# Spreading ScalarE's work on the next pair's samples over more attention steps, and asking for its function tables early

One core of a Trainium2 chip; the metric is the device time of one execution, in microseconds (us). Engines are named as in the profile: PE is TensorE, DVE VectorE, ACT ScalarE, POOL GpSimd. All runs quoted are of the fast state.

## What is computed

Four layers on x of shape (2, 512, 32, 32). The change touches the first, a deformable attention whose bias is a small network over every (query, key) pair. Cut to what matters:

```python
off  = gelu(conv6x6(q) + b);  off = tanh(off @ pw) * 4        # per pair of heads: 64 sample points
kv   = grid_sample(xn, grid + off)                            # bilinear samples  -> "samples"
pos  = grid_q - grid_kv
bias = sign(pos) * log1p(abs(pos))                            # Sign, Abs, Ln
bias = relu(bias @ cpb_w1); bias = relu(bias @ cpb_w2)        # 128 x 128, for 1024 x 64 pairs a head
sim  = q @ k + bias @ cpb_w3
out  = softmax(sim) @ v                                       # Exp
```

The other three layers (an MLP with Gelu and three ordinary attentions) come after it, and the change does not touch them.

## The kernel before

The attention runs over 8 pairs of heads (t), each in 64 steps. A step fills two z tiles (16 matmuls) and evacuates both with ACT. The work of the *next* pairs is a chain of Python generators, `behind`: after each step's z work, one `next(behind)` emits what stands up to the next `yield`. In the traces ACT runs its instructions in the order in which the program emits them (h at 494.94 us, near at 496.05, wx at 497.18, wy at 497.68, the next h at 498.81), so whatever is emitted there stands on ACT between the last evacuation of this step and the first of the next.

```python
ps_s = ...tile_pool(name="att_ps_s", bufs=1, space=PSUM)   # sim
ps_z = ...tile_pool(name="att_ps_z", bufs=3, space=PSUM)   # z, and every other PSUM tile of the attention
def zt(shape, name): return ps_z.tile(shape, F32, name=name, tag="z")

def second(h1s):                                 # one step
    for part in range(2):
        z = zt([P, HW], "z")
        ...                                      # 8 matmuls in the trace (4 pairs) of 128x512
        h2 = ...
        nc.scalar.activation(h2, z, AF.Relu, bias=b2h[:, part:part+1])      # "h<-z"

def offsets(t):
    qpad = one.tile([P, 36, 36], F32, name="qpad", tag="pixels")
    nc.gpsimd.memset(qpad, 0.0)
    ...                                          # pq -> qpad, 36 taps on DVE over 24 steps
    for h in range(2): nc.scalar.activation(act[r, r], accf[r], AF.Gelu, ...)
    yield
    po = zt([P, 2], "po"); ...; nc.scalar.activation(th, po, AF.Tanh)
    yield
    ...                                          # nxy, pos, gp on DVE
    yield
    nc.scalar.activation(sgn, pos, AF.Sign); nc.scalar.activation(pos, pos, AF.Abs)
    nc.scalar.activation(pos, pos, AF.Ln, bias=1.0)
    yield

def samples(t):
    gpb = zt([P, 2, P], "gpb"); ...              # holds a z buffer
    yield
    for ax in range(2):
        nc.scalar.activation(near[:, ax, :], ir, AF.Abs, ...)
        nc.scalar.activation(near[:, ax, :], near[:, ax, :], AF.Relu, ..., accum_out=...)
    nc.vector.tensor_mul(wsum[:, 2:3], wsum[:, 0:1], wsum[:, 1:2])
    nc.scalar.activation(wx, gpb[:, 0, :], AF.Abs, bias=cs("px"))
    nc.scalar.activation(wx, wx, AF.Relu, bias=1.0, scale=-1.0)
    for k in range(8):
        nc.scalar.activation(wy[:, k, :], gpb[:, 1, :], AF.Abs, bias=cs("py", k))
        if k % 4 == 3: yield
    nc.scalar.activation(wy, wy, AF.Relu, bias=1.0, scale=-1.0)
    ...

def finish(t, sim):
    nc.scalar.activation(simb, sim, AF.Identity, bias=simbias[t])
    yield
    pt = zt([P, 8, P], "pt"); ...                # 8 transposes; holds a z buffer
    nc.vector.tensor_reduce(mx, ptv, AX.X, ALU.max, negate=True)
    yield
    for g in range(16):
        nc.scalar.activation(atv[:, g, :], ptv[:, g, :], AF.Exp, bias=mx[:, g:g+1], accum_out=...)
        if g % 4 == 3: yield
    ...
```

Of the kernel before, what the change touches and what calls it, by code (L numbers as in the profile page):

```python
# [11 lines left out]
F32 = mybir.dt.float32  # L12
AF = mybir.ActivationFunctionType
# [5 lines left out]
P = 128  # L19
# [60 lines left out]
def kernel(ctx: ExitStack, tc: tile.TileContext, a: dict, out: bass.AP):  # L80
    nc = tc.nc
# [10 lines left out]
    def col(name, i=0, n=1):  # L92
        lo = _PC_AT[name][0] + i
        return pc[:, lo : lo + n]

    def cs(name, i=None):
        lo, hi = _CONST_AT[name]
        return cst[:, lo:hi] if i is None else cst[:, lo + i : lo + i + 1]
# [34 lines left out]
    def accumulate(pm, pairs):  # L133
        for k, (w, m) in enumerate(pairs):
            nc.tensor.matmul(pm, w, m, start=(k == 0), stop=(k == len(pairs) - 1))  # L135

    def layer0(l0, fold_d, t2_b, o2_b):

        l0.enter_context(in_order(tc))
        one = l0.enter_context(tc.tile_pool(name="att1", bufs=1))  # L140
# [9 lines left out]
        def zt(shape, name):  # L150
            return ps_z.tile(shape, F32, name=name, tag="z")
# [100 lines left out]
            nc.vector.tensor_tensor(cpb_w2, cpb_w2, pw3, ALU.mult)  # L252


        gps = {}

        def offsets(t):
            b, pr = divmod(t, NPAIR)
            qpad = one.tile([P, 36, 36], F32, name="qpad", tag="pixels")
            nc.gpsimd.memset(qpad, 0.0)  # L260
            pq = zt([P, HW], "pq")
            for half in range(2):
                n = slice(half * HALF, (half + 1) * HALF)
                nc.tensor.matmul(pq[:, n], qws[:, pr, :], xs[b][:, pr, n], start=True, stop=True)
            yield
            nc.scalar.activation(
                qpad[:, 1:33, 1:33], pq.rearrange("p (y x) -> p y x", x=W), AF.Identity, bias=qb[:, pr : pr + 1]
            )
            yield

            qv = qpad.rearrange("p (a i) (c k) -> p a i c k", i=4, k=4)
            acc = one.tile([P, HD, WD], F32, name="acc")
            for tap in range(36):
                ky, kx = divmod(tap, 6)
                src = qv[:, ky // 4 : ky // 4 + HD, ky % 4, kx // 4 : kx // 4 + WD, kx % 4]
                w = col("dw_w", tap)
                if tap == 0:
                    nc.vector.tensor_scalar(acc, src, w, None, ALU.mult)
                else:
                    nc.vector.scalar_tensor_tensor(acc, src, w, acc, ALU.mult, ALU.add)  # L280
                if tap % 3 != 1:
                    yield
            accf = acc.rearrange("p y x -> p (y x)")
            act = actbd[t % 2]
            for h in range(2):
                r = slice(h * DH, (h + 1) * DH)
                nc.scalar.activation(act[r, r], accf[r], AF.Gelu, bias=col("dw_b")[r])
            yield
            po = zt([P, 2], "po")
            nc.tensor.matmul(po, act, col("pw_w", 0, 2), start=True, stop=True)  # L290
            th = two.tile([P, 2], F32, name="th")
            nc.scalar.activation(th, po, AF.Tanh)
            yield

            nxy = two.tile([P, 2], F32, name="nxy")
            nc.vector.scalar_tensor_tensor(nxy, th, 4.0, cs("gxy"), ALU.mult, ALU.add)
            nc.vector.tensor_scalar(nxy, nxy, 2.0 / 7.0, -1.0, ALU.mult, ALU.add)

            pos = two.tile([P, 2, 32], F32, name="pos")
            nc.vector.tensor_tensor(  # L300
                pos,
                cs("gq").unsqueeze(1).to_broadcast([P, 2, 32]),
                nxy.unsqueeze(2).to_broadcast([P, 2, 32]),
                ALU.subtract,
            )
            gp = two.tile([P, 2], F32, name="gp")
            nc.vector.tensor_scalar(gp, nxy, 1.0, W / 2.0, ALU.add, ALU.mult)
            nc.vector.tensor_scalar(gp, gp, -0.5, None, ALU.add)
            gps[t] = gp
            yield  # L310
            sgn = two.tile([P, 2, 32], F32, name="sgn")
            nc.scalar.activation(sgn, pos, AF.Sign)
            nc.scalar.activation(pos, pos, AF.Abs)
            nc.scalar.activation(pos, pos, AF.Ln, bias=1.0)
            yield
            nc.vector.tensor_mul(pos, pos, sgn)
            nc.sync.dma_start(out=slog_d[t].rearrange("x p i -> p x i"), in_=pos)
            tables.add(t)
# [12 lines left out]
        def samples(t):  # L331
            b, pr = divmod(t, NPAIR)
            xt = one.tile([P, 8, P], F32, name="xt", tag="pixels")
            nc.sync.dma_start(
                out=xt, in_=a["xt"][b, :, pr * P : (pr + 1) * P].rearrange("(k p) c -> p k c", p=P)
            )

            gp = gps.pop(t)
            gpb = zt([P, 2, P], "gpb")
            for ax in range(2):  # L340
                nc.tensor.matmul(
                    gpb[:, ax, :], gp[:, ax : ax + 1].to_broadcast([P, P]), ident, start=True, stop=True
                )
            yield

            near = two.tile([P, 2, 32], F32, name="near")
            wsum = two.tile([P, 3], F32, name="wsum")
            for ax in range(2):
                nc.scalar.activation(near[:, ax, :], ir, AF.Abs, bias=gp[:, ax : ax + 1], scale=-1.0)
                nc.scalar.activation(  # L350
                    near[:, ax, :], near[:, ax, :], AF.Relu, bias=1.0, scale=-1.0, accum_out=wsum[:, ax : ax + 1]
                )
            nc.vector.tensor_mul(wsum[:, 2:3], wsum[:, 0:1], wsum[:, 1:2])
            wx = one.tile([P, P], F32, name="wx")
            nc.scalar.activation(wx, gpb[:, 0, :], AF.Abs, bias=cs("px"))
            nc.scalar.activation(wx, wx, AF.Relu, bias=1.0, scale=-1.0)
            wy = one.tile([P, 8, P], F32, name="wy")
            for k in range(8):
                nc.scalar.activation(wy[:, k, :], gpb[:, 1, :], AF.Abs, bias=cs("py", k))
                if k % 4 == 3:  # L360
                    yield
            nc.scalar.activation(wy, wy, AF.Relu, bias=1.0, scale=-1.0)
            yield
            nc.gpsimd.tensor_tensor(wy, wy, wx.unsqueeze(1).to_broadcast([P, 8, P]), ALU.mult)
            for _ in range(4):
                yield

            pk = zt([P, 2, P], "pk")
            accumulate(pk[:, 0, :], [(xt[:, k, :], wy[:, k, :]) for k in range(8)])
            accumulate(pk[:, 1, :], [(wsum[:, 2:3].to_broadcast([P, P]), ident)])  # L370
            yield
            shift = one.tile([P, P], F32, name="shift")
            nc.scalar.mul(shift, pk[:, 1, :], col("bn1_b", pr))
            kv = kvbd[t % 2]
            for h in range(2):
                r = slice(h * DH, (h + 1) * DH)
                nc.vector.scalar_tensor_tensor(
                    kv[r, r], pk[r, 0, r], s1[r, pr : pr + 1], shift[r, r], ALU.mult, ALU.add
                )
            yield  # L380
            pkv = zt([P, 2, P], "pkv")
            nc.tensor.matmul(pkv[:, 0, :], kq_w[:, pr, :], kv, start=True, stop=True)
            nc.tensor.matmul(pkv[:, 1, :], kv, bd["vw"][:, pr, :], start=True, stop=True)
            kq = one.tile([P, P], F32, name="kq")
            nc.scalar.copy(kq, pkv[:, 0, :])
            kqs[t] = two.tile([P, P], F32, name="kqs")
            nc.scalar.mul(kqs[t], pkv[:, 0, :], s1q[:, pr : pr + 1])
            vbd[t] = two.tile([P, P], F32, name="vbd")
            nc.scalar.copy(vbd[t], pkv[:, 1, :])
            yield  # L390
            pb = zt([P, 1], "pb")
            nc.tensor.matmul(pb, kq, b1q[:, pr : pr + 1], start=True, stop=True)
            simbias[t] = two.tile([P, 1], F32, name="simbias")
            nc.vector.tensor_add(simbias[t], pb, col("cpb_b3"))
# [86 lines left out]
        def finish(t, sim):  # L481
# [5 lines left out]
            simb = two.tile([P, HW], F32, name="simb", tag="simb")  # L487
            nc.scalar.activation(simb, sim, AF.Identity, bias=simbias[t])
            yield
            pt = zt([P, 8, P], "pt")  # L490
            for i in range(8):
                nc.tensor.transpose(pt[:, i, :], simb[:, i * P : (i + 1) * P], ident)
# [93 lines left out]
        key_steps = key_weights()  # L586
        advance(key_steps)
        steps = offsets(0)
        advance(steps, 26)
        drain(key_steps)  # L590
# [736 lines left out]
    with ExitStack() as l0:  # L1327
        w1 = layer0(l0, fold_d, t2_b, o2_b)
# [92 lines left out]
```

## Time and profile before

| | before |
|---|---|
| median of 3 runs | 3727.63 us (3726.69 to 3728.03) |
| PE busy | 3675.3 of 3725.8 us |
| attention of layer 0, first to last z matmul | 55.4 to 2205.1 us |
| PE's waits of z for ACT's evacuation | 26.6 us, 23 times |

The share of busy time says that PE is full; it does not say what a change can still win. That stands in the list of PE's waits, and the chain of work shows where each wait sits: as long as PE bounds, the chain is one long piece "PE z", and where ACT lines break into it, PE stood still. The prediction shows those lines.

### The profile page before, as it was taken

The page shows a single profiled execution, that of the slowest core. Times are in us where ns is not written, and L with a number is a line of the kernel's source. Part 1 is how long each engine was busy: PE and PEld are TensorE (multiplying, and loading weights), DVE is VectorE, ACT ScalarE, POOL GpSimd, SP SyncE. Part 2 cuts the span into 40 slices and gives each one's busy share as a digit, 9 for nine tenths or more (in the row PEclk, how much of TensorE's full clock was granted, in tenths as well). Part 3 has the DMA queues.
Part 4 walks back from the last instruction along what each step waited for, and adds up shares of the span by engine and source line. Part 5 has one row for each costly group of instructions (what it writes and reads, how often), then busy time and mean ns, then how long its engine had stood idle before and what let it go on. Part 6 is the DMA issues. An engine that isn't in the chain of part 4 may idle for free.

```text
span 3725.8 us, 37390 instructions
## 1 busy us (share of the span) xinstructions
PE 3675.3 (99%) x15234; PEld 1342.1 (36%) x15234; DVE 2371.8 (64%) x2317; ACT 1586.4 (43%) x1940; POOL 478.6 (13%) x188
## 2 busy tenths in 40 slices
PE   9999999999999999999999999999999999999999
PEld 4333333333333333333333334444433333444443
DVE  6988998998996998998998960000036447030222
ACT  4655566565664566656656541100134234111111
POOL 1112122122121012121132210000001000000000
PEclk9999999999999999999999999999999999999999
DMA  4100012001010110010101001000100000000000
GB/s 149 24 15 14 18 24 62 17 20 18 18 23 12 13 23 18 18 24 12 24 18 22 18 2 51 9 34 12 57 1 1 1 1 0 14 0 0 6 29 24
DMA packets 96852, 78.42 MB, mean 21 GB/s; under 512 B 10656, under 2 KB 84768, under 8 KB 95904
## 3 DMA queue, kind: packets, MB, share of 16 engines
q1 hardware_dynamic: 96528, 75.41, 8.3%
q8 instruction: 123, 2.02, 0.2%
q14 instruction: 57, 0.47, 0.0%
q10 hardware_dynamic: 144, 0.52, 0.0%
HBM read 64.12 MB, written 10.75 MB: 20 GB/s over the span
## 4 chain that ended last, share of the span: by engine, by line
PE 93%; DVE 3%; ACT 3%; issue 0%; DMA 0%; POOL 0%; SPq 0%; DVEq 0%; POOLq 0%; ACTq 0%
PE z L443 44%; PE sim L465 6%; PE pw L135 6%; PE ph L991 6%; PE pp L1002 6%; PE pm L1026 5%; PE pmv L135 4%; PE score L1130 3%; PE score L135 3%; PE pv L1178 3%; PE ppr L1057 2%; PE pp L549 1%; ACT h L451 1%; DVE h L425 1%; DVE h L456 1%; PE pf L135 1%
## 5 line engine op out<-in xcount | busy, mean ns | idle before, releaser
L443 PE MATMUL z<-h,cpb_w 128*64 128x512 f32 x8192 | 1788.7, 594 | 28.5 <-ACT h L451 26.6
L451 ACT ACTIVATE h<-z,b2h 128x1024 f32<-128x1024 f32 x1024 | 1137.8, 1114 | 868.0 <-PE z L443 858.7
L425 DVE CUSTOM_DVE_ANT_1 h<-tab,tab 128x1024 f32<-128x1024 f32 x1024 | 1221.8, 1234 | 121.1 <-PE z L443 120.7
L443 PEld LDWEIGHTS z<-h,cpb_w 128*64 128x64 f32 x8192 | 575.6, 137 | 1208.9 <-issue 1107.5
L456 DVE SCALAR_TENSOR_TENSOR h<-h,turn,h 128x1024 f32<-128x1024 f32 x512 | 689.6, 1347 | 5.3 <-ACT h L451 5.3
L410 POOL TENSOR_SCALAR tab<-tab,pc 128x512 f32<-128x512 f32 x63 | 270.9, 4300 | 1576.3 <-DMA tab<-slog_d 1116.3
L1005 DVE SCALAR_TENSOR_TENSOR x<-pp,pc,x 128x512 f32<-128x512 f32 x16 | 12.0, 749 | 375.8 <-PE pp L1002 375.8
L465 PE MATMUL sim<-h,w 128*32 128x512 f32 x2048 | 234.3, 595 | 0.7 <-DVE h L456 0.7
L135 PE MATMUL pw<-p,vT 128*128 128x512 f32 x512 | 221.8, 593 | 1.3 <-DVE y L1236 1.3
L991 PE MATMUL ph<-xn,wa 128*128 128x512 f32 x512 | 220.9, 593 | 1.4 <-POOL xn L975 1.4
L1002 PE MATMUL pp<-hid,wb 128*128 128x512 f32 x512 | 220.4, 592 | 0.0
L1131 ACT ACTIVATE p<-score 128x1024 f32<-128x1024 f32 x144 | 139.5, 1021 | 156.8 <-PE score L1130 156.8
L1068 DVE TENSOR_TENSOR acc<-acc,p 128x2048 f32<-128x2048 f32 x56 | 129.6, 2315 | 105.1 <-ACT p L1131 57.8
L994 ACT ACTIVATE hid<-ph,pc 128x512 f32<-128x512 f32 x64 | 44.0, 687 | 332.6 <-PE ph L991 332.6
L953 POOL TENSOR_SCALAR hc<-x,sc,sh 128x1024 f32<-128x1024 f32 x16 | 29.0, 1822 | 902.3 <-DVE sh L949 870.1
L1070 DVE TENSOR_TENSOR acc<-p 128x2048 f32<-128x2048 f32 x12 | 27.5, 2291 | 182.2 <-ACT p L1265 108.8
L991 PEld LDWEIGHTS ph<-xn,wa 128*128 128x128 f32 x512 | 97.1, 190 | 123.2 <-issue 120.4
L1002 PEld LDWEIGHTS pp<-hid,wb 128*128 128x128 f32 x512 | 97.4, 190 | 122.4 <-issue 122.4
L135 PEld LDWEIGHTS pw<-p,vT 128*128 128x128 f32 x512 | 97.1, 190 | 122.5 <-issue 120.9
L411 POOL TENSOR_SCALAR tab<-tab,pc 128x512 f32<-128x512 f32 x63 | 131.1, 2081 | 16.3 <-DMA tab<-slog_d 16.2
L1130 PE MATMUL score<-q,k 64*128 64x512 f32 x512 | 127.2, 615 | 0.0
L1026 PE MATMUL pm<-hc,wa 128*64 128x512 f32 x512 | 122.5, 604 | 0.0
(217 smaller groups left out, 2044.5 us busy)
## 6 DMA issues: line engine op xcount, KB each, us to landing
tab<-slog_d SPq DMA_DIRECT2D x128, 256.0 KB, 6.3
wa<-in_qkv_w SPq DMA_DIRECT2D x8, 768.0 KB, 6.8
xt<-in_xt SPq DMA_DIRECT2D x8, 512.0 KB, 3.8
wa<-in_mlp_w SPq DMA_DIRECT2D x4, 1024.0 KB, 17.0
wb<-in_mlp_w SPq DMA_DIRECT2D x16, 256.0 KB, 5.4
x_d<-x SPq DMA_DIRECT2D x16, 256.0 KB, 2.0
out<-x SPq DMA_DIRECT2D x16, 256.0 KB, 2.0
wa<-in_proj_w SPq DMA_DIRECT2D x8, 256.0 KB, 9.0
```

The source lines that it names most:

```text
L135: nc.tensor.matmul(pm, w, m, start=(k == 0), stop=(k == len(pairs) - 1))
L410: engine.tensor_scalar(tabs[0], tabs[0], col("cpb_w1", 0), col("cpb_b1"), ALU.mult, ALU.add)
L425: nc.vector._custom_dve(TENSOR_ADD_SAT, out=h1, in0=tx[:, quad, ri, :].unsqueeze(1).to_broadcast([P, H, W]), in1=ty[:, quad, ri, :].unsque ...
L443: nc.tensor.matmul(z[point * 64 : point * 64 + 64, n], cpb_w2[:, part * 64 : part * 64 + 64], h1s[point][:, n], start=True, stop=True,)
L451: nc.scalar.activation(h2, z, AF.Relu, bias=b2h[:, part : part + 1])
L456: nc.vector.scalar_tensor_tensor(parts[0], parts[0], turn, parts[1], ALU.mult, ALU.add)
L465: nc.tensor.matmul(sim[quad * 32 : quad * 32 + 32, n], w3[:, lo : lo + 32], h2[:, n], start=(r == 0 and j < 4), stop=False,)
L991: nc.tensor.matmul(ph, w1[:, k, m * P : (m + 1) * P], xn_now[:, k, :], start=(k == 0), stop=(k == CC - 1))
L1002: nc.tensor.matmul(pp, w2[:, k, m * P : (m + 1) * P], h1[:, k, :], start=(k == 0), stop=(k == HID // P - 1))
L1026: nc.tensor.matmul(pm[at : at + wide], w[:, k, lo + at : lo + at + wide], h[k][:, n], start=(k == 0), stop=(k == CC - 1),)
L1130: nc.tensor.matmul(sc[:, part, :], ks[part][r, left[part]], qs[part][r, n], start=True, stop=True)
L1131: nc.scalar.activation(p[:, :, n], sc, AF.Exp, scale=scale)
```

## The change

Its intent: ACT's stretches of work between two evacuations become shorter, so that none is long enough to let PE run out of free z buffers. The samples' activations are spread over five steps in place of three. The tables for Gelu, Ln and Exp are asked for one to three steps ahead, by a one-column activation on a scratch tile, `table(...)`, before which the compiler puts the table load.

```diff
+        trial = one.tile([P, 2], F32, name="trial")
+        nc.gpsimd.memset(trial, 1.0)
+
+        def table(function):
+            nc.scalar.activation(trial[:, 1:2], trial[:, 0:1], function)
 ...  offsets(t)
+                if tap == 33:
+                    table(AF.Gelu)
                 if tap % 3 != 1:
                     yield
 ...
             gps[t] = gp
+            table(AF.Ln)
             yield
 ...  samples(t)
             nc.vector.tensor_mul(wsum[:, 2:3], wsum[:, 0:1], wsum[:, 1:2])
+            yield
             wx = one.tile([P, P], F32, name="wx")
 ...
-                if k % 4 == 3:
+                if k % 3 == 1:
                     yield
 ...  finish(t, sim)
             yield
+            table(AF.Exp)
             pt = zt([P, 8, P], "pt")
```

## The prediction

> **What bounds the kernel now.** I read the page's busy shares first, then the slices, the view of who waited for whom, the chain that ended last in two short windows, and the groups of ScalarE.
>
> TensorE (PE) is busy 3675.3 of 3725.8 us, so in the whole program only about 50 us can be won by filling its gaps. The change touches the first part alone, the bias attention of layer 0 (55 to 2206 us, 512 steps of two z tiles each). The waits of PE, longest first, begin so:
>
> ```profile
> PE z L443 <- ACT h L451: 26.6, 23, 1.6
> PE den L1085 <- DVE acc L1068: 3.4, 2, 2.2
> PE den L135 <- ACT r L1100: 2.7, 4, 0.7
> PE pwarm L160 <- ACT warm L157: 2.3, 1, 2.3
> PE z L443 <- ACT qpad L266: 1.9, 1, 1.9
> ```
>
> Columns: total us, times, longest. 23 waits of the z matmuls for ScalarE's (ACT) evacuation h carry more than half of all PE idle time; nothing else in the attention comes near. Where are they? The chain that ended last shows two kinds in one period of 266.7 us (one of the eight pairs of heads). The first is in the samples:
>
> ```profile
> 491.28 3.63 PE z L443 x16
> 494.92 0.02 issue
> 494.94 1.11 ACT h L451
> 496.05 0.22 ACT near L349
> ...
> 497.18 0.26 ACT wx L355
> ...
> 497.68 1.12 ACT wy L359 x4
> 498.81 1.01 ACT h L451
> 499.82 0.04 issue
> ```
>
> Between two evacuations ACT does near, wx and four wy; PE sits until the h after them frees a z buffer, at 499.86. The second is in the softmax (start us, us, what):
>
> ```profile
> 603.70 1.11 ACT h L451
> 604.82 0.02 issue
> 604.83 1.28 ACT L501
> 606.12 0.01 issue
> 606.13 1.02 ACT at L501 x7
> ...
> 607.42 1.01 ACT h L451
> 608.43 0.04 issue
> ```
>
> "ACT L501" with no tile is the table load for Exp. A third, the same with Gelu's load at 473.36 and two Gelu activations, is in the offsets. The groups of ACT count the loads that the change is about:
>
> ```profile
> L314 ACT ACT_TABLE_LOAD x8 | 10.3, 1283 | 0.1
> L287 ACT ACT_TABLE_LOAD x7 | 9.0, 1283 | 0.1
> L501 ACT ACT_TABLE_LOAD x7 | 9.0, 1283 | 0.1
> ```
>
> I then read the timeline at each place and took the distance between starts of neighbouring PE matmuls over the usual 0.43 us: samples 8 times 1.73 us; Exp 7 times 1.58, and 0.16 once more in its later steps; Gelu 6 times 0.79 (the seventh falls beside the sim matmuls); Ln 2 times 0.33. Sum 13.8 + 12.2 + 4.7 + 0.7 = 31.4 us. The wait list agrees: 26.6 us, plus 23 times 0.163 us, because a matmul's modelled 0.592 us overhangs its 0.43 us spacing, plus the seven small ones of 0.16, is 31.5. That is the ceiling of the gain: 0.84% of the time.
>
> **What the Trainium skill says.** "ScalarE: Activation LUTs", section "What ACT_TABLE_LOAD costs", gives about 1283 ns for the load and about 1380 ns of drain with it. The trace agrees on the load (1283 ns) but shows no drain: load at 604.83, next activation at 606.13. So I charge 1.28 us for a load. The same page, "Table sets: the hidden batching unit", says that cheap functions such as relu, copy, identity and abs are in every set; in the trace h (Relu) runs between loads without a reload, so a load asked for two steps early is not undone by the h in between. "PSUM — Partial Sum Buffer", "Specifications (TRN2)", has eight banks of 512 fp32 per partition: a z tile of 1024 takes two, the program has three z buffers and one sim, and the memory is full. "Perfetto Trace Analysis", "Optimization Strategy", reads consistent bubbles as a lack of buffers: here the bubbles recur at the same three places of each period.
>
> **How a stall arises.** PE fills a z tile in 1.72 us (128 matmuls, 16 tiles, take 27.62 us, less 0.16 of overhang). h starts 0.23 us after the fill, runs 1.11, and PE goes on 0.06 later: 1.40 us from fill to free. ACT is idle 0.60 us between two h. With three buffers PE may run two fills on, so the slack is 3.43 - 1.40 = 2.03, and extra work X between two h stalls PE only if it exceeds 0.60 + 2.03 = 2.63 us. But gpb, pt and po are tiles of the same three buffers, and while one lives the slack is 1.72 - 1.40 = 0.32: X may be 0.92. Check on before: samples X = 2.73 gives 1.81 (read: 1.73); Exp X = 2.5 gives 1.6 (read: 1.58). So the size of X and the state of the buffers explain what I see.
>
> **The change, part by part.** Built, both programs have the same number of table loads; the changed one gains 24 one-column activations (8 each of Gelu, Ln, Exp, some 0.2 us by the 0.17 to 0.25 of ACT's smallest rows) and one small memset; PE, VectorE (DVE) and the queues keep their instructions, later by two steps from wy on.
>
> 1. Samples. The 2.73 us become 1.14 (near), 1.12 (wx, two wy), 0.8 and 0.8 (three wy each), one group a step, gpb held two steps longer. First group: 1.14 - 0.92, about 0.2 of stall. That stall shifts PE against ACT, so the second group, no larger, adds nothing; a step has 3.43 us for 2.23 of h, so 1.20 is free and every group fits. Left 0.2 of 1.73: saved 1.5 x 8 = 12.2.
> 2. Exp. The load goes one step up, where pt is not yet taken and PE's eight transposes (1.02 us) give ACT more room: ACT was idle 1.78 us there. X = 1.5, no stall. Each of the four steps keeps X = 1.2 with pt held: 2.23 + 1.2 is just the step, so some 0.2 at the first and the 0.16 of before at a later one remain, about 0.4 of 1.74. Saved 1.3 x 7 = 9.3, just the load.
> 3. Gelu. Load plus trial, X = 1.5, two steps ahead with three buffers: under 2.63. Then X = 0.7 with po: under 0.92. Saved 0.75 x 6 = 4.5.
> 4. Ln: likewise 0.6 in all. In the prologue PE is busy with the folds up to the first z at 55.36, so nothing there; the last pair's Exp needs no load before or after.
>
> Sum: 12.2 + 9.3 + 4.5 + 0.6 = 26.6 us. All lie on PE, which is the chain, so they count in full: 3727.6 - 26.6 = 3701. As nearly every unforeseen thing makes it less, I say 3702.
>
> **The rivals.** *VectorE becomes the bound.* In the period from 606.5 to 873.2 us DVE is busy 244.85 of 266.70 us; with PE's period shortened by 3.6 it would be 93%. Over the taps of the offsets DVE needs more per step (3.7 plus half a us) than PE gives (3.9 with sim's share), and its lead before the z matmuls, read as the distance from the end of h1 to PE's start, sinks from over 5 to 1.7 us there, and to 1.4 us after the samples; one could fear that 1.5 us less of PE stall makes it nil. Against it: before the taps DVE waits for PE for 6.4 us at 630 to 641, so it starts them with full buffers anyhow; and the 2.1 us that GpSimd's wy product costs DVE (one 3.38 us join at 773.19) comes two steps later too. If it does bite, up to 1 us a period comes back: 3710. *The wait only moves.* ACT has the same work and 24 trials more. If my thresholds were wrong by half a us, each early load would stall PE by that; 22 of them, 11 us: 3712. The check of the thresholds at two places speaks against it, and ACT is busy only 160.68 us of the 266.70. *gpb held longer makes a new wait.* Two more steps on two buffers, perhaps 0.2 each: 3 us, 3705. *All stalls go*: 3696, which needs the Exp steps to fit with no rest.
>
> **Range and chances.** 3702 us, 8 in 10 between 3698 and 3710: the low end is nearly no rest at the samples and Exp, the high end is DVE biting in each period. The ceiling of 31.4 us is 0.84%, so a gain over 2% is excluded by the trace as I read it, and a loss over 2% would need 3.3 us of new stall at each of the 22 places. Faster 0.01, same 0.98, slower 0.01.
>
> **What would show it.** Right: PE's wait of z for h falls from 26.6 us to 2 to 5, PE idle by some 23; the period becomes about 263.1 us; table loads still 8, 7, 7 but before tile trial; PE goes without a gap past wx and past the Exp load, with rests of about 0.2 at near and the first exp. Wrong: z waits on DVE h L425, or sim on the join, of more than 2 us in total (the first rival); gaps beside the trial loads (the second); gaps of 0.2 or more at each wy group (the third); a load more than before per period.

## The result

| | before | after |
|---|---|---|
| median | 3727.4 us (4 runs, 3726.69 to 3728.03) | 3701.84 us (4 runs, 3700.96 to 3704.68) |
| ratio of fast runs | | 0.9933, 95% interval 0.9916 to 0.995 |
| the same again, other chip time | 3727.97 us (9 runs) | 3701.4 us (5 runs), ratio 0.993 |

Ratios are the mean time of one kernel's fast runs over that of the other's of the same rounds, so not quite the ratio of the medians quoted. 25.6 us were saved (26.6 the second time), under the 2% line: "same" by verdict, and 3701.84 against 3702 predicted.

PE's waits in the changed kernel, in the same view that opened the prediction (total us, times, longest):

```profile
PE z L454 <- ACT qpad L273: 3.5, 1, 3.5
PE den L1097 <- DVE acc L1080: 3.4, 2, 2.2
```

The line of 26.6 us is gone whole, and no wait for a DVE tile took its place. The groups of ACT now hold the loads under the line of `table`:

```profile
L259 ACT ACT_TABLE_LOAD x22 | 28.2, 1283 | 0.4
L259 ACT ACTIVATE trial<-trial 128x1 f32<-128x1 f32 x24 | 4.8, 202 | 0.2
```

22 loads as before (8 + 7 + 7), of the same 1283 ns, and 24 trials of 0.2 us: 4.8 us more on ACT, though its busy time in the page grows by 1.9 only (1586.4 to 1588.3). No wait of PE in the list is for them. The chain that ended last, in the windows that hold Exp's load and the Gelu, Ln and samples of one period:

```profile
596.44 1.02 PE pt L504 x8
597.47 14.74 PE z L454 x65
...
738.26 0.31 PE po L299 x2
738.57 10.45 PE z L454 x48
749.02 0.64 PE gpb L351 x4
749.66 3.57 PE sim L476 x32
753.23 21.77 PE z L454 x100
```

Where ACT lines broke into the chain before (Exp's load, near to wy), PE now runs through. ACT around Exp's load, in the timeline (start, duration, idle before):

```profile
596.49 1.11 ACT L462 ACTIVATE h<-z,b2h 128x1024 f32<-128x1024 f32 x1 [0.28 <-PE z L454]
597.62 1.28 ACT L259 ACT_TABLE_LOAD   x1
598.92 0.20 ACT L259 ACTIVATE trial<-trial 128x1 f32<-128x1 f32 x1
599.38 1.11 ACT L462 ACTIVATE h<-z,b2h 128x1024 f32<-128x1024 f32 x1 [0.26 <-PE z L454]
```

The load fits between two evacuations, with 0.26 us to spare before the next z is full: the time in which PE makes pt's transposes.

One line got longer: the first evacuation's wait on qpad, 1.9 us before and 3.5 here. That profile was also the slowest of the four runs (3704.68), and in it PE's mean granted clock is 0.57 from 72 to 76 us, right after that wait; in the second job's profile (3701.39) the wait is 2.2 and the clock doesn't fall there. In that one the attention takes 2123.12 us from first to last z matmul, against 2149.69 before: 26.57 us less. The prologue (55.7 against 55.4 us) and the rest after the last z matmul (1520.8 us in both) are alike, so all of the gain is in the attention, and its size is the predicted 26.6; that it agrees to the tenth is luck, as shown below.

### The profile page after: what moved, and what is told of

It is laid out like the page before. It is cut to its first block, busy times and chain, and to the rows that moved or that the text cites. A ratio compares the mean times of both kernels' runs of the same rounds, so it can differ in the third digit from the quotient of the medians.

```text
span 3702.9 us, 37416 instructions
## 1 busy us (share of the span) xinstructions
PE 3677.3 (99%) x15234; PEld 1339.8 (36%) x15234; DVE 2369.3 (64%) x2317; ACT 1588.3 (43%) x1964; POOL 500.1 (14%) x189
## 4 chain that ended last, share of the span: by engine, by line
PE 98%; DVE 1%; ACT 0%; DMA 0%; issue 0%; POOL 0%; SPq 0%; DVEq 0%; POOLq 0%; ACTq 0%
PE z L454 48%; PE sim L476 6%; PE pw L135 6%; PE ph L1003 6%; PE pp L1014 6%; PE pm L1038 5%; PE pmv L135 5%; PE score L1142 3%; PE score L135 3%; PE pv L1190 3%; PE ppr L1069 2%; PE pp L561 2%; PE pf L135 1%; PE pk L135 0%; DVE acc L1080 0%; PE pv L539 0%
## 5 line engine op out<-in xcount | busy, mean ns | idle before, releaser
L421 POOL TENSOR_SCALAR tab<-tab,pc 128x512 f32<-128x512 f32 x63 | 294.8, 4679 | 1621.7 <-DMA tab<-slog_d 1309.4
L422 POOL TENSOR_SCALAR tab<-tab,pc 128x512 f32<-128x512 f32 x63 | 129.1, 2049 | 20.8 <-DMA tab<-slog_d 20.6
```

Source lines behind the costliest of these rows:

```text
L421: engine.tensor_scalar(tabs[0], tabs[0], col("cpb_w1", 0), col("cpb_b1"), ALU.mult, ALU.add)
```

## The experiments

My theory: PE stalls by X - 0.92 us when another tile holds one of the three z buffers and by X - 2.63 when none does, X being ACT's extra work between two evacuations. Rivals: a stall depends on the amount of ACT work alone; an early load only moves its wait; a step's spare ACT time (1.2 us) is the limit. Each edit is against the kernel named.

### The loads alone

Against the changed kernel:

```diff
             nc.vector.tensor_mul(wsum[:, 2:3], wsum[:, 0:1], wsum[:, 1:2])
-            yield
-                if k % 3 == 1:
+                if k % 4 == 3:
```

> The three early table loads alone, on the kernel before; the samples stay in three steps. My theory (each stall is set by the extra ScalarE work between two evacuations and by the number of free z buffers): PE's gaps at Exp, Gelu and Ln go, the eight of 1.73 us at wx and wy stay. Saved 7 x 1.5 + 6 x 0.72 + 0.7 = 15 us, so 3712 us. Rival (an early load only moves its wait): gaps beside the trial loads, 3724 to 3727.

Measured: 3712.22 us against 3727.59 before (ratio 0.996, 0.9947 to 0.9974). PE's wait of z for h, in the list of waits:

```profile
PE z L453 <- ACT h L461: 12.5, 8, 1.6
```

Eight waits are left of 23, the samples'. The early loads save 15.4 us by the time (14.7 by the attention's length in its trace, 2134.98 us) and move no wait.

### The spread alone

Against the kernel before: the added `yield` and `k % 3 == 1` only.

> The samples' activations over five steps, and no early loads. My theory: the eight gaps of 1.73 us shrink to 0.1 each, all others stay: 8 x 1.6 = 13 us saved, 3714.5 us. With the run of the loads alone the two parts should add up to the whole change within 2 us. Rival (spread holds the gpb buffer two steps longer and so makes new gaps): half of that, 3720.

Measured: 3717.29 us (0.9974, 0.9961 to 0.9988), 10.3 us saved, less than the 13 expected. The list of waits has

```profile
PE z L444 <- ACT h L452: 14.2, 15, 1.4
```

so the eight at the samples are gone (8 + 15 = 23). In its trace the attention is 12.1 us shorter than before, but starts 1.7 us later: PE's mean granted clock from 26 to 42 us, in the prologue, was 0.79 and not 0.89. I can show that for the profiled run only. The two parts add up to 15.4 + 10.3 = 25.7 us, the whole change to 25.6. As single times of one kernel differ by 2 to 3 us, the traces are the better check: by the attention's length 14.7 + 12.1 = 26.8 us against 26.6. The parts act at different places, and I see no sign that they help or hinder each other.

### More work, but a free buffer

Against the kernel before:

```diff
+            gpc = one.tile([P, 2, P], F32, name="gpc")
+            nc.scalar.copy(gpc, gpb)
-            nc.scalar.activation(wx, gpb[:, 0, :], AF.Abs, bias=cs("px"))
+            nc.scalar.activation(wx, gpc[:, 0, :], AF.Abs, bias=cs("px"))
-                nc.scalar.activation(wy[:, k, :], gpb[:, 1, :], ...)
+                nc.scalar.activation(wy[:, k, :], gpc[:, 1, :], ...)
```

> The kernel before, with gpb copied out of PSUM by one more activation at the head of the samples, so that its z buffer is free while wx and wy are made. ScalarE has 0.4 us more work in the very step that stalls. My theory (two buffers: stall = X - 0.92; three: X - 2.63): X = 3.1 stalls 0.5 us instead of 1.73, 8 x 1.2 = 10 us saved, 3717.5 us. Rival (the amount of work between two evacuations alone decides): each stall grows by 0.4 us, 3730.5 us.

Measured: 3719.53 us (0.9977, 0.9963 to 0.999). ACT has more to do in the stalling step, and the kernel is 8 us *faster*. The chain there:

```profile
759.77 1.11 ACT h L453
760.89 0.26 ACT gpc L347
...
762.83 1.27 ACT wy L361 x4
764.10 1.01 ACT h L453
765.11 0.04 issue
765.15 4.93 PE z L445 x21
```

X grew from 2.6 to 3.1 us, and PE's gap fell from 1.73 to 0.46 us (0.5 expected). This decides against "the amount of work alone": part of the stall's cause is that gpb, a tile of 1 KB per partition, sits in a z buffer while ACT works from it. 8 x 1.27 = 10.1 us were in the gaps, 8.5 in the attention's length (2141.19 against 2149.69 us) and 8.1 in the time; the rest I didn't find.

### Exp's load put back

Against the changed kernel:

```diff
-            table(AF.Exp)
             pt = zt([P, 8, P], "pt")
 ...
+            table(AF.Exp)
             at = two.tile([P, 8, P], F32, name="at", tag="simb")
```

> The changed kernel with Exp's trial and load put back directly before the first Exp, so that the load is with four Exps in one step and pt is held. My theory: X = 1.28 + 0.2 + 1.2 = 2.7 with two buffers, a gap of 1.8 us in place of 0.16 at seven places: 11.5 us lost of the gain, 3713.5 us. Rival (it is the separate trial, or fewer steps per load, and not the place, that helps): it stays at 3702.

Measured: 3711.42 us (0.9955, 0.9941 to 0.9968). The chain of before is back, with a trial in it:

```profile
603.06 1.11 ACT h L462
604.17 0.02 issue
604.19 1.28 ACT L259
605.47 0.01 issue
605.48 0.20 ACT trial L259
605.68 0.82 ACT at L513 x6
...
606.86 1.01 ACT h L462
607.88 0.04 issue
```

Seven gaps of 1.67 us. The same instructions one step later cost 10 us: it is the place of the load that matters, not its being a separate instruction.

### The threshold, by needless work

Against the changed kernel, n activations of 128x256 at one step of seven periods, where nothing else holds a z buffer:

```diff
+        idle = one.tile([P, 256], F32, name="idle")
 ...
+                if tap == 15 and t > 0:
+                    for _ in range(n):
+                        nc.scalar.activation(idle, cst[:, 0:256], AF.Identity)
```

n = 7: 

> The changed kernel with seven needless 128x256 activations (about 0.3 us each, so X near 2.1 us) put in one step of the offsets of seven periods, where no other tile holds a z buffer. My theory (three free buffers: X stalls PE only above 2.63 us): no gap at all, time as the changed kernel, 3702 us within the noise. Rival (a step leaves ScalarE 1.2 us and all above it is lost): 0.9 us x 7 = 6 us more, 3708.

n = 12: 

> The same with twelve needless activations, X near 3.6 us. My theory: a gap of X - 2.63, about 1.0 us at each of seven places, 7 us more, 3709. Rival: 2.4 us x 7 = 17 us more, 3719. The size of the gap in the trace, with X read from the same trace, is the test of the threshold.

n = 10: 

> Ten needless activations in place of twelve, about 0.43 us each, X = 4.27. By the line through seven and twelve (gap = X - 2.65) a gap of 1.6 us at seven places, 11.4 us over the changed kernel, 3713. The twelve cost 23 us where their gaps sum to 17.4; theory of that difference: after a PE gap of more than some 2 us the granted clock drops for some us, in some executions. Then this run, with gaps below 2 us, costs its gaps alone: 3713. Rival (something else grows with the needless work): more than 3716.

n = 16: 

> Sixteen, X = 6.8, gaps of 4.2 us at seven places: 29 us by the gaps alone, 3731. If the clock drops after each such gap and that costs 1.6 us, as after the 3.7 us gap of the changed kernel's first profile, 40 us: 3742, and the trace shows PE's clock near 0.57 for 4 us after each. Rival: 3731, and the clock stays.

I had taken 0.3 us an activation; in the trace they don't overlap and start 0.45 us apart, so X was larger than expected, and the times expected for n = 7 and 12 (3702 and 3709 us) rested on a wrong X: only the threshold is tested, with X from the trace. X below is read from the timeline (start of the next h, less the end of the one before), the gap from the distance of neighbouring PE matmul starts over 0.43 us.

| where | buffers | X | PE gap | X - gap | median us |
|---|---|---|---|---|---|
| samples, before | 2 | 2.63 | 1.73 | 0.90 | 3727.4 |
| Exp, before | 2 | 2.49 | 1.58 | 0.91 | |
| Exp's load put back | 2 | 2.58 | 1.67 | 0.91 | 3711.42 |
| first Exp, after | 2 | 1.06 | 0.16 | 0.90 | 3701.84 |
| gpb copied | 3 | 3.12 | 0.46 | 2.66 | 3719.53 |
| n = 7 | 3 | 2.90 | 0.25 | 2.65 | 3702.93 |
| n = 10 | 3 | 4.25 | 1.60 | 2.65 | 3712.89 |
| n = 12 | 3 | 5.14 | 2.49 | 2.65 | 3724.78 |
| n = 16 | 3 | 6.94 | 4.28 | 2.66 | 3744.33 |

Two thresholds, 0.90 and 2.65 us, over very different work; I had worked out 0.92 and 2.63. They are 1.75 us apart, about one fill of a z tile (1.72). The rival of the spare 1.2 us a step is out: n = 7 puts 2.9 us into a step, by which the rival would lose 7 x 1.7 = 12 us, and the gaps in its trace sum to 1.8 us, the time is 1.1 longer.

The time agrees with the gaps up to n = 10 (7 x 1.6 = 11.2 us of gaps, 11.1 in the time). At n = 12 and 16 it exceeds them: 22.9 us against 17.4, 42.5 against 30. The stretches of n = 16 around one gap show why, in the view of busy time by stretch (PEclk, the granted clock, is third from the end of each row):

```profile
685.00:698.20 13.20, 9.08 (x44) 2.77 (x40) 13.13 (x15) 10.95 (x21) 4.17 (x2) 1.00 0.12 29
698.20:702.20 4.00, 4.00 (x16) 0.92 (x20) 2.24 (x4) 2.52 (x3) 0.00 (x0) 0.57 0.00 0
702.20:706.00 3.80, 3.80 (x36) 1.03 (x30) 3.53 (x5) 0.56 (x1) 0.00 (x0) 1.00 0.00 0
```

Over the 4 us after the gap the mean granted clock is 0.57; asked more finely, it is 0.50 from 698.56 to 701.97 us, so PE loses half of 3.4, some 1.7 us. Each of the seven gaps of n = 16 has such a stretch of 3.4 us (some begin inside the gap; the last is 6.8 long). The stretch after a gap of n = 10:

```profile
685.90:690.00 4.10, 4.09 (x32) 1.22 (x36) 4.07 (x6) 3.08 (x3) 0.00 (x0) 1.00 0.00 0
```

No drop. 7 x (4.28 + 1.7) = 42 us is the cost of n = 16. At n = 12 the profiled run, the fastest of the five, shows the drop after one of seven gaps of 2.5 us; the timed ones, at mean clocks of 0.996 to 0.998 where n = 10 has 0.998 to 0.999, presumably have more. Their places I can't show.

### The last gaps

Against the changed kernel; the second run also has the second edit:

```diff
-            nc.gpsimd.memset(qpad, 0.0)
+            (nc.vector if t == 1 else nc.gpsimd).memset(qpad, 0.0)
 ...
-                if g % 4 == 3:
+                if g % 3 == 2:
```

> The largest gap left in the changed kernel: the first evacuation of the attention waits on qpad, whose clearing on GpSimd stands behind a table's product that waits for its DMA. Here VectorE clears that one qpad. The gap of 2.0 to 3.7 us at 68 us goes; with it the drop of PE's granted clock after it (0.57 for 4 us in the changed kernel's profile). 2 to 5 us saved: 3698. If another wait stands behind it (h1 tables of the second chunk, DVE now later by 1 us): same as the changed kernel.

> The same and three Exps a step instead of four, so X = 0.9 with pt held, under 0.92: the seven rests of 0.16 and 0.1 us go, 1.8 us more saved, 3696. Rival (pt held two steps longer costs something): no faster than the run before.

Measured: 3700.28 us (0.9925) and 3699.16 us (0.9924), against 3702 for the change and 3698 and 3696 expected: most of what the gaps promised did not come. Then the second of them beside the changed kernel on one chip:

> The changed kernel once more, as the yardstick on the same chip for the run beside it: 3702 us as before. Its first gap, at qpad, should again be 2.0 or 3.7 us.

> Qpad cleared by VectorE and three Exps a step, beside the changed kernel on the same chip. By the gaps that its trace lost: 2.0 at least at qpad, 7 x 0.16 + 7 x 0.1 at the Exps, 4 us less than the changed kernel, 3698. If the timed difference is under 1 us, the gaps' sum doesn't show in the time and something gives it back.

Measured: 3701.4 us (3701.19 to 3703.44) for the change, 3700.21 (3698.01 to 3701.99) with both edits; by ratio 0.993 and 0.9924, intervals that overlap. The wait on qpad and every gap over 0.13 us at the Exps are gone from its trace, and its attention is 3.3 us shorter (2119.83 against 2123.12). But the prologue ends 1.9 us later (57.6 against 55.7). The stretches there, first of the changed kernel, then with both edits:

```profile
26.00:42.00 16.00, 14.19 (x62) 8.83 (x62) 9.01 (x29) 4.71 (x10) 0.00 (x0) 0.89 0.47 84
```

```profile
26.00:42.00 16.00, 14.20 (x52) 8.82 (x51) 9.28 (x29) 3.92 (x9) 0.00 (x0) 0.79 0.43 78
```

PE is as busy, at a clock of 0.79 and not 0.89. Of the fourteen profiles six show 0.89 there, seven 0.79 and one 0.68, that is one, two or three times 3.4 us at half the clock, 1.7 us lost each time; no edit of mine comes that early on PE, and all three profiles with qpad on VectorE show 0.79. The same happens far behind the attention, at the longest wait of PE's den matmuls for DVE's acc (at some 3112 to 3157 us, a gap of 2.34 us in every profile): in nine of the fourteen the clock then is 0.50 for 3.4 us, in five it isn't. So 1.7 us come and go between runs at places that no edit touches. Whether the 0.79 with qpad on VectorE is chance I leave open, so no version is shown to beat the change: 1 us, not resolved.

## Why the prediction was right

- **The ceiling.** The 31.4 us of gaps at 30 places (23 of them waits in the list, seven small) was the quantity that bounded the gain, and 26.6 us of it came. It was read a little high: against the same matmuls in the changed kernel, Gelu's places were 0.72 us each and not 0.79 (the first z matmul started 0.90 us after po's last and now starts 0.18 after it), Ln's 0.24 and not 0.33, so 30.8 us. In the changed kernel's first profile 159 ns is left at seven places and about 0.1 us at fifteen.
- **How a stall arises.** The thresholds worked out beforehand, 0.92 and 2.63 us, hold within 0.03 us at the nine places of the table; two of these, samples and Exp before, had served as their check. This step carried the whole forecast; the copy of gpb shows that the buffers are in it and not only the work. The check's X of 2.73 at the samples was 0.1 too large (2.63 by the timeline), which is why it gave 1.81 where 1.73 was read.
- **Samples.** 1.5 us each was forecast and 1.63 came (a rest of 0.10 and not 0.2): X of near is 1.03 and not 1.14, as ACT's instructions overlap by 0.1 (near starts 0.1 us before h ends). By the trace of the spread alone 12.1 us, 12.2 forecast; by its time 10.3.
- **Exp, Gelu, Ln.** Forecast 9.3 + 4.5 + 0.6 = 14.4, with the loads alone 15.4 by the time and 14.7 by the trace. The mis-sized term is Exp's rest: 0.16 + 0.10 us, at the first and third step, and not 0.4, so Exp gave 7 x 1.48 = 10.4 and not 9.3. No run moved Gelu's or Ln's load alone; their 4.3 and 0.5 us are read from the gaps.
- **What was to be seen.** The wait of z for h was to fall to 2 to 5 us and fell out of the list; rests so short hide in the overhang of a matmul's modelled end. The period was to be 263.1 us and is 263.06.
- **The rivals.** VectorE did not become the bound: in the prediction's period its smallest lead over PE in the taps is 1.73 us where it was 1.75, since it enters them with a lead of some 10 us as argued. After the samples the smallest lead is 1.91 us, not 1.44; the smallest of the whole attention is 1.07, where it was 1.01. The loads brought no wait of their own, and gpb's longer life none above 0.1 us.
- **Not foreseen, and luck.** The gaps taken away sum to 28.2 us and not 26.6 (samples 13.0, Exp 10.4, Gelu 4.3, Ln 0.5), and the attention is 26.57 us shorter: 0.4 of the 1.6 us between went to the longer wait on qpad, about 0.5 to five more changes between z and sim matmuls (0.52 us from start to start where two z matmuls have 0.42), the rest I didn't find. So terms sized too small and this loss happened to cancel; the mechanism was right, the agreement to 0.2 us was luck. And the prologue's clock and the wait on qpad move the time by 1 to 4 us between runs: as much as the last gaps are worth.

## What to carry to other kernels

Where one engine fills buffers and another empties them, work slipped in on the emptying engine is free up to a threshold that can be worked out from three durations (fill, empty, idle between) and the number of buffers *free at that moment*, and costs its full excess above it (here more from gaps of 2.5 us on, where PE's clock fell). So split and place such work by the state of the buffers: a table load in the step before a tile takes a buffer is free, and one step later it cost some 1.5 us here, all of load and trial; and a small tile in a large ring costs a whole buffer as long as it lives. What is left to win is bounded by the sum of the bounding engine's gaps, counted from the trace before a line is changed.

## What the Trainium skill lacked or had wrong

- "ScalarE: Activation LUTs", section "What ACT_TABLE_LOAD costs", gives a drain of about 1380 ns with each load: here the load took 1283 ns, and the next activation started 0.01 to 0.02 us after it (loads at 604.83 and 597.62 us), so a switch cost 1.3 us and not 2.66.
- The same page: it does not say that a load can be asked for steps ahead by a one-column activation (202 ns). 22 such loads, placed well, saved 15.4 us.
- "TensorE: Matmul & The Clock Gate", section "HAM oscillation — how this bites in real kernels", warns of PE-idle gaps over about 3.4 us. Here PE's clock was halved for 3.4 us after, or from within, all seven gaps of 4.28 us (n = 16) and the one of 3.66 us, but also at one of seven gaps of 2.49 us (n = 12) and, behind the attention, at a gap of 2.34 us in nine of fourteen profiles; at the gaps of 1.73 us and less in the attention never. So a gap under that section's figure can cost a drop.
- No page has the rule for how much work fits between two evacuations: 0.90 us with two free buffers and 2.65 us with three, at a fill of 1.72 us and 1.11 us of evacuation.
